# Later slots, an eighth row buffer and a shorter hand-over in a fused conv-attention and mixture-of-experts kernel

## The chip, the core and the metric

One core of a Trainium2 chip runs the kernel. The metric is device time in microseconds (us) of one execution. TensorE is PE in the profile (PEld are its weight loads), VectorE is DVE, ScalarE is ACT, GpSimd is POOL and SyncE is SP. SP only issues DMAs; POOL issues the indirect ones, which scatter or add rows by an index. Each engine and each issuing queue works strictly in order.

## The reference

The input is x of shape (4, 256, 64, 64) in float32, 16384 pixels of 256 channels. Layer 0 adds a 3x3 neighbourhood attention; layer 1 adds a sliding-window attention over tokens and a mixture of experts. What matters here is the mixture:

```python
def _moe(tokens, router_w, w1, b1, w2, b2):
    logits = tokens @ router_w.T
    probs = softmax(logits)
    rw, re = top_k(probs, 2)
    rw = rw / rw.sum(-1, keepdims=True)
    combine = zeros((N, 8)).at[arange(N)[:, None], re].set(rw)
    out = tokens
    for e in range(8):
        h = gelu(tokens @ w1[e] + b1[e], approximate=False)
        out = out + combine[:, e:e + 1] * (h @ w2[e] + b2[e])
    return out

x = x + conv_attention(group_norm(x))
t = to_tokens(x)
t = t + windowed_attention(layer_norm(t))
t = t + moe(layer_norm(t))
```

## The kernel before

The pixels are 32 blocks of 512 tokens (`NB` = 32, eight an image). Two streams run at once.

The **stream of blocks** runs a loop over steps g = 0 to 33. In step g four generators are interleaved: `produce(g + 1)` (queries, scores), `attend(g)` (attention of layer 0, whose first PE work is the transpose `ptp` at L688), `tail(g - 1)` (window attention, norm, choice of experts) and `ranks(g - 2)`. `tail` stores the block's tokens to `out` with SP (`store`, L749). `ranks` counts where each token goes and scatters each token's normed row to `rows_in` in HBM, once for each of its two experts: eight indirect DMAs of 128 rows a block, issued by POOL at L1001.

The **stream of slots** (`experts`) does the mixture for the first 28 blocks. They form 15 groups, numbered from 0: 13 of two blocks, then two of one (`GROUPS`). A group's rows are cut into slots of 256 rows of one expert, 105 in all; group 0 gives 1 slot, groups 1 to 12 give 8 each, the last two 4 each, so the first slots of groups 1 to 5 are 1, 9, 17, 25 and 33. A slot m goes through these steps:

- `fetch` (L1171): SP reads the slot's 256 rows from `rows_in` into a row buffer `sx` of pool `rowp`. It waits until all rows of its group are scattered, and until the buffer is free.
- `matrix`, `pixels`, `hidden`, `output`: the expert's weights are copied by ACT (L1188), the rows transposed on PE (`ptx`, L1195, four instructions), multiplied (`psh`, L1207, and `psy`, L1225, eight each), and bias and gate are applied in place by DVE (L1229, L1230).
- `add` (L1243): the slot's sum. POOL adds the rows into `out` with two indirect DMAs of 128 rows. A sum waits for the landing of the sum before it, and for the group's stores. It frees the row buffer.

A slot is fetched two slots ahead of its transposes. `rowp` has seven buffers, so slot m uses the buffer of slot m - 7. The scattering DMAs are not issued at once: they are put into the list `waiting`, and each sum hands out four or two of them behind itself (`give_rows`); a fetch hands out what is left of its group.

How far the slots have come at each point of the block loop is set by `follow`: at time `at` (in steps) it lets the slots run up to `due`, the lower of two lines of straight pieces, `most` and `wanted`. `most` says that group k begins at `begins[k]`, which is two steps and a lag after the group's last block.

Engines' orders come from the program's order with priorities, so giving out a slot later moves its instructions on every engine.

The last four blocks (28 to 31) are the **tail**: their rows are cut into 53 half slots of 128 rows (`halves`: fetch L1319, transposes L1334, products L1344 and L1360), 21 of which also hold what was left over of the earlier groups. Half slots write their products with POOL to an intermediate `sums_a` (L1373); the 21 add to `out` (L1390). The sums of the last slots of `experts` are held (`HELD` = 4) and put between these, one for every two half slots. At the end `together` reads `sums_a`, adds two rows for each token (L1448) and stores the four blocks.

Of the kernel before, what the change touches and what calls it, by code (L numbers as in the profile page):

```python
# [62 lines left out]
def hybrid_block_kernel(ctx: ExitStack, tc: tile.TileContext, ins: dict, out: bass.AP):  # L63
# [9 lines left out]
    NB = B * NBI  # L73
# [19 lines left out]
    NS = NB - 4  # L93
    GROUPS = (*[2] * 13, *[1] * 2)
    assert sum(GROUPS) == NS
    first_of = [sum(GROUPS[:k]) for k in range(len(GROUPS))]
    where = [(k, j) for k, n in enumerate((*GROUPS, NB - NS)) for j in range(n)]
    APART = len(GROUPS)
# [25 lines left out]
    w2p = ctx.enter_context(tc.tile_pool(name="w2p", bufs=2))  # L124
    w3p = ctx.enter_context(tc.tile_pool(name="w3p", bufs=3))
    w4p = ctx.enter_context(tc.tile_pool(name="w4p", bufs=4))
    rowp = ctx.enter_context(tc.tile_pool(name="rowp", bufs=7))
    w1sp = ctx.enter_context(tc.tile_pool(name="w1sp", bufs=3))
    hbm = ctx.enter_context(tc.tile_pool(name="hbm", bufs=1, space=bass.MemoryType.DRAM))
    ps_a = ctx.enter_context(tc.tile_pool(name="ps_a", bufs=4, space=PSUM))  # L130
# [522 lines left out]
    wxs, sums, table, norm1, x1c = {}, {}, {}, {}, {}  # L653
# [470 lines left out]

    ready = []
    adds = []
    HELD, owed = 4, []
    waiting, given_rows = [], []

    def in_turn(inst, others, own):  # L1130

        for d in others:
            tc.add_manual_dep(
                inst, d.name,
                mybir.DependencyInfo(
                    mybir.DependencyClass.NoSync, mybir.DependencyReason.SCHED_ONLY
                ),
                reason="order of the indirect transfers",
            )
        own.append(inst)  # L1140

    def give_rows(n, k=None):

        while waiting and (n > 0 or k is not None and waiting[0][0] <= k):
            waiting.pop(0)[1]()
            n -= 1

    def experts():
# [86 lines left out]
        def add(m, xs):  # L1235
            k, n = of[m]

            behind = adds[-U:]
            if n == 0:
                at = 1 + sum(GROUPS[:k])  # L1240
                behind = behind + stored[0 if k == 0 else at : at + GROUPS[k]]
            for t in range(U):
                inst = nc.gpsimd.indirect_dma_start(  # L1243
                    out=out, out_offset=bass.IndirectOffsetOnAxis(
                        ap=xs[:, t, C + E : C + E + 1].bitcast(U32), axis=0
                    ),
                    in_=xs[:, t, 0:C], in_offset=None, compute_op=ALU.add,
                ).ins
                tc.declare_no_dep(
                    inst, group="stores", keep=behind, reason="rows of a later group's blocks"  # L1250
                )
                tc.declare_no_dep(
                    inst, group="adds", keep=behind, reason="behind the slot before, no other"
                )
                for d in behind:
                    tc.add_manual_dep(
                        inst, d.name,
                        mybir.DependencyInfo(
                            mybir.DependencyClass.Sync, mybir.DependencyReason.DATA
                        ),  # L1260
                        reason="sums of one row",
                    )
                tc.add_to_no_dep_group("adds", inst)
                in_turn(inst, given_rows[-2:], [])
                adds.append(inst)
            give_rows(4 if len(waiting) > 4 else 2)

        raw = {m: fetch(m) for m in range(FETCH)}
        xcs, hs, done = {}, {}, {}
        for m in range(-2, total + 1):  # L1270
            if FETCH <= m + 2 + FETCH < total:
                raw[m + 2 + FETCH] = fetch(m + 2 + FETCH)
            if m + 2 < total:
                xcs[m + 2] = matrix(m + 2), pixels(m + 2, raw[m + 2])
            yield
            if 0 <= m + 1 < total:
                hs[m + 1] = expert_of(m + 1), hidden(m + 1, *xcs.pop(m + 1))
            yield
            if m > 0:
                sum_ = lambda m=m, xs=done.pop(m - 1): add(m - 1, xs)  # L1280
                if m - 1 < total - HELD:
                    sum_()
                else:
                    owed.append((2.0, sum_))
            if 0 <= m < total:
                yield from output(m, *hs.pop(m), raw.pop(m))
# [171 lines left out]


    STEPS, LAG = {NB: 17, NB + 1: 12}, 0.35  # L1460
    begins = [at + 2 + LAG for at in first_of[1:]] + [NS + 2.0]
    most = [(at, max(0, n - FETCH - 1)) for at, n in zip((*begins, NB + 2.0), (*first_slot, first_slot[-1]))]
    wanted = [(begins[1], 1), *((NB + n, first_slot[-1] - m) for n, m in ((0, 11), (1, 7), (2, 3)))]
    stream, done = experts(), 0
# [17 lines left out]
    for g in range(NB + 2):  # L1482
# [10 lines left out]
        n = 0  # L1493
# [75 lines left out]
```

## Time and profile before

| | |
|---|---|
| median of 3 runs | 1234.81 us (1232.86 to 1239.05) |
| profiled execution | 1238.46 us, of which the span is 1236.8 |
| PE busy | 1106.7 us, 89% of the span |
| DVE, ACT, POOL busy | 917.1, 857.0, 699.5 us |
| sums (L1243), 210 DMAs | 332.9 us of POOL, 1585 ns each |
| rows scattered (L1001), 256 DMAs | 254.6 us of POOL, 995 ns each |
| mean granted clock of TensorE | 0.970 |
| first `sums_a` of the tail (L1373) | at 1081.99 us |

In a line of the timeline the columns are the start in us, the length in us, engine, line, operation, output and inputs, the count, and in brackets the engine's idle time before it with what ended it. In the view by lines, the numbers behind the count are busy us, the mean length in ns, and idle us before with what ended it. In the view of waits they are us in total, times, and the longest. In the windows each engine has its busy us and count; the number behind POOL's count is the granted clock, then come the share of the DMA engines and GB/s. A clock of 1 is full speed.

### The profile page before, as it was taken

The page shows a single profiled execution, that of the slowest core. Times are in us where ns is not written, and L with a number is a line of the kernel's source. Part 1 is how long each engine was busy: PE and PEld are TensorE (multiplying, and loading weights), DVE is VectorE, ACT ScalarE, POOL GpSimd, SP SyncE. Part 2 cuts the span into 40 slices and gives each one's busy share as a digit, 9 for nine tenths or more (in the row PEclk, how much of TensorE's full clock was granted, in tenths as well). Part 3 has the DMA queues.
Part 4 walks back from the last instruction along what each step waited for, and adds up shares of the span by engine and source line. Part 5 has one row for each costly group of instructions (what it writes and reads, how often), then busy time and mean ns, then how long its engine had stood idle before and what let it go on. Part 6 is the DMA issues. An engine that isn't in the chain of part 4 may idle for free. (4 is left out here: it accounts for less than half of the span.)

```text
span 1236.8 us, 29028 instructions
## 1 busy us (share of the span) xinstructions
PE 1106.7 (89%) x8762; PEld 791.4 (64%) x8762; DVE 917.1 (74%) x4632; ACT 857.0 (69%) x1752; POOL 699.5 (57%) x642
## 2 busy tenths in 40 slices
PE   5888889999997969999998999999999999688880
PEld 4544556777775747777666766766666677577670
DVE  4589878888886857888886878888888889234443
ACT  1467679878886757787786887787777766266660
POOL 3113316556553565675665666666566668577772
PEclk9999999999998989999999999999999999799995
DMA  8895548666668577777746786676566456655557
GB/s 277 273 317 172 179 144 244 180 150 157 157 174 159 137 187 199 193 191 198 188 115 163 186 214 166 160 207 156 134 155 154 104 112 148 129 132 118 131 128 233
DMA packets 136146, 214.01 MB, mean 173 GB/s; under 512 B 16368, under 2 KB 102400, under 8 KB 131768
## 3 DMA queue, kind: packets, MB, share of 16 engines
q1 hardware_dynamic: 86264, 137.00, 36.1%
q0 software_dynamic: 48352, 73.05, 29.5%
q10 hardware_dynamic: 1376, 2.10, 0.5%
q8 instruction: 73, 1.20, 0.4%
q14 instruction: 81, 0.66, 0.2%
HBM read 120.78 MB, written 91.31 MB: 171 GB/s over the span
## 5 line engine op out<-in xcount | busy, mean ns | idle before, releaser
L1243 POOL DMA_INDIRECT out<-sx x210 | 332.9, 1585 | 277.8 <-DVE sx L1230 51.3
L1001 POOL DMA_INDIRECT rows_in<-tok,rows x256 | 254.6, 995 | 125.3 <-issue 78.8
L1225 PE MATMUL psy<-w,h 128*128 x840 | 214.1, 386 | 0.4 <-issue 0.2
L1207 PE MATMUL psh<-xc,w1s 128*128 128x256 f32 x840 | 206.2, 387 | 0.0
L1225 PEld LDWEIGHTS psy<-w,h 128*128 128x128 f32 x840 | 153.3, 191 | 50.9 <-issue 24.9
L1207 PEld LDWEIGHTS psh<-xc,w1s 128*128 128x128 f32 x840 | 153.4, 192 | 35.4 <-issue 10.3
L1229 DVE TENSOR_TENSOR sx<-psy,b2b 128x256 f32<-128x256 f32 x210 | 87.7, 417 | 66.3 <-PE psy L1225 60.2
L576 PE MATMUL psq<-x,qks 128*128 128x512 f32 x256 | 124.0, 606 | 1.8 <-ACT qks L497 1.8
L734 PE MATMUL pso<-mixT,vo 128*128 128x512 f32 x256 | 123.5, 605 | 0.0
L1213 ACT ACTIVATE h<-psh,w1s 128x256 f32<-128x256 f32 x210 | 88.1, 471 | 32.0 <-PE psh L1207 30.9
L1195 PE MATMUL ptx<-ident,sx 128*128 128x128 f32 x420 | 66.4, 281 | 31.9 <-DMA sx<-rows_in 31.8
L1199 ACT COPY xc<-ptx 128x512 f32<-128x512 f32 x105 | 61.1, 582 | 47.5 <-PE ptx L1195 47.0
L1195 PEld LDWEIGHTS ptx<-ident,sx 128*128 128x128 f32 x420 | 50.9, 146 | 57.2 <-issue 41.3
L1230 DVE TENSOR_SCALAR sx<-sx 128x256 f32<-128x256 f32 x210 | 78.5, 374 | 2.0
L1213 ACT ACT_TABLE_LOAD x59 | 75.7, 1283 | 0.8
L893 ACT ACTIVATE x<-x,scale 128x256 f32<-128x256 f32 x120 | 63.2, 590 | 18.3 <-DVE scale L867 16.4
L584 ACT ACTIVATE q<-psq,qbb,irc 128x512 f32<-128x512 f32 x64 | 49.9, 779 | 33.1 <-PE psq L576 27.6
L780 PE MATMUL psp<-wpr,x1c 128*128 128x136 f32 x512 | 70.2, 282 | 0.7 <-DVE ispread L473 0.7
L780 PEld LDWEIGHTS psp<-wpr,x1c 128*128 128x128 f32 x512 | 65.5, 190 | 4.8 <-issue 2.1
L576 PEld LDWEIGHTS psq<-x,qks 128*128 128x128 f32 x256 | 45.8, 193 | 34.9 <-issue 33.5
L734 PEld LDWEIGHTS pso<-mixT,vo 128*128 128x128 f32 x256 | 45.5, 190 | 34.3 <-issue 30.1
L1188 ACT COPY w1s<-w1b 128x514 f32 x105 | 65.1, 627 | 2.1 <-issue 0.2
(277 smaller groups left out, 2494.7 us busy)
## 6 DMA issues: line engine op xcount, KB each, us to landing
xp<-in_xp SPq DMA_DIRECT2D x32, 1024.0 KB
sx<-rows_in SPq DMA_DIRECT2D x105, 272.0 KB
x<-in_x SPq DMA_DIRECT2D x32, 660.0 KB
xs<-in_xs SPq DMA_DIRECT2D x32, 512.0 KB
out<-x SPq DMA_DIRECT2D x28, 512.0 KB
sxa<-rows_in SPq DMA_DIRECT2D x32, 136.0 KB
rows_in<-tok,rows POOLq DMA_INDIRECT x256
out<-sx POOLq DMA_INDIRECT x210
```

Source lines behind the costliest of these rows:

```text
L576: inst = nc.tensor.matmul(ps.rearrange("p (r w) -> p r w", w=W), qks[:, ci, co * P : (co + 1) * P], t[:, ci, 1 : TH + 1, 1 : W + 1], start ...
L734: nc.tensor.matmul(ps, vo[:, ci, co * P : (co + 1) * P], mixT[:, ci, :], start=(ci == 0), stop=(ci == NC - 1),)
L780: nc.tensor.matmul(ps[:, u, :], xc[:, ci, t * P : (t + 1) * P], wpr[:, ci, :], start=(ci == 0), stop=(ci == NC - 1),)
L1001: return nc.gpsimd.indirect_dma_start(out=rows_in[:, :], out_offset=bass.IndirectOffsetOnAxis(ap=rows[:, c, t : t + 1], axis=0), in_=tok[: ...
L1188: nc.scalar.copy(w1s, w1b[:, e, :])
L1195: nc.tensor.transpose(pt[:, c, t * P : (t + 1) * P], xs[:, t, c * P : (c + 1) * P], ident)
L1207: nc.tensor.matmul(ps[:, f, :], w1s[:, o : o + P], xc[:, ci, :], start=(ci == 0), stop=(ci == NC - 1),)
L1213: inst = nc.scalar.activation(h[:, f, :], ps[:, f, :], AF.Gelu, bias=w1s[:, F1 + f : F1 + f + 1])
L1225: nc.tensor.matmul(ps, h[:, f, t * P : (t + 1) * P], w2[:, e, f, :], start=(f == 0), stop=(f == NC - 1),)
L1229: nc.vector.tensor_add(ys[:, t, :], ps, b2b[:, e, :])
L1230: nc.vector.tensor_scalar_mul(ys[:, t, :], ys[:, t, :], xs[:, t, bass.ds(e + C, 1)])
L1243: inst = nc.gpsimd.indirect_dma_start(out=out, out_offset=bass.IndirectOffsetOnAxis(ap=xs[:, t, C + E : C + E + 1].bitcast(U32), axis=0), ...
```

## The change

Four numbers or conditions change; no instruction is added to the program or taken out of it.

```diff
-    rowp = ctx.enter_context(tc.tile_pool(name="rowp", bufs=7))
+    rowp = ctx.enter_context(tc.tile_pool(name="rowp", bufs=8))
...
-    HELD, owed = 4, []
+    HELD, owed = 3, []
...
-            give_rows(4 if len(waiting) > 4 else 2)
+            give_rows(4 if len(waiting) > 4 or APART in ready or NB - 1 in sums else 2)
...
-    begins = [at + 2 + LAG for at in first_of[1:]] + [NS + 2.0]
+    begins = [at + 2 + min(LAG * max(n, 1), 1.05) for n, at in enumerate(first_of[1:])] + [NS + 3.0]
```

- `begins`: the lag stays 0.35 of a step for groups 0 and 1, is 0.70 for group 2 and 1.05 from group 3 on; the last knot is at step 31, not 30. In the orders of instructions of both kernels, most of slots 4 to 56 stand later among the blocks on PE than before, and from slot 57 on PE's order is the same.
- `rowp`: eight row buffers, so slot m uses the buffer of slot m - 8.
- `give_rows`: once the last block's ranks are known, a sum hands out four rows. The last block's last four scattering DMAs now stand behind one sum, that of slot 98, where two stood behind 98's and two behind 99's.
- `HELD`: three slots' sums are held for the tail, not four, so the sum of slot 101 stands ahead of the first `sums_a`.

## The prediction

> **What bounds the kernel now.** I read the page's section 1 first, then PE's groups in the view by lines:
>
> ```profile
> PE 1106.7 (89%) x8762; PEld 791.4 (64%) x8762; DVE 917.1 (74%) x4632; ACT 857.0 (69%) x1752; POOL 699.5 (57%) x642
> ```
>
> ```profile
> L1195 PE MATMUL ptx<-ident,sx 128*128 128x128 f32 x420 | 66.4, 281 | 31.9 <-DMA sx<-rows_in 31.8
> ```
>
> PE is busy for 1106.7 of 1236.8 us, and no other engine passes 917.1, so the question is where PE stands idle (last column of the second line). 31.8 us of it stand before the first step of a slot (its transposes, L1195), ended by the fetch of that slot's rows. The timeline of PE gives the large ones:
>
> ```profile
> 380.25 1.09 PE L1195 MATMUL ptx<-ident,sx 128*128 128x128 f32 x4 [6.26 <-DMA sx<-rows_in]
> ...
> 463.04 1.09 PE L1195 MATMUL ptx<-ident,sx 128*128 128x128 f32 x4 [10.38 <-DMA sx<-rows_in]
> ...
> 1059.12 1.09 PE L1195 MATMUL ptx<-ident,sx 128*128 128x128 f32 x4 [8.30 <-DMA sx<-rows_in]
> ```
>
> Counting L1195 in fours, these are slots 25, 33 and 104 (counted from 0). 25 and 33 are the first slots of groups 4 and 5 (counted from 0; group 3 is the fourth). Two smaller waits, 1.36 us at 123 and 4.41 at 168, are slots 0 and 1, which the change does not touch; 0.94 at 436.5 is slot 31. SyncE's waits between 340 and 390, and between 440 and 465, say what the fetches of 25 and 33 waited for:
>
> ```profile
> SPq L1171 <- DMA rows_in<-tok,rows: 19.1, 3, 17.7
> ...
> SPq L1171 <- DMA rows_in<-tok,rows: 17.2, 2, 15.9
> ```
>
> The rows of the group's last block had not been scattered yet. Lastly the windows, whose column behind POOL is the granted clock:
>
> ```profile
> 350.00:400.00 50.00, 43.69 (x343) 30.20 (x341) 35.86 (x190) 36.44 (x72) 25.92 (x22) 0.93 0.71 151
> 400.00:450.00 50.00, 48.84 (x416) 36.07 (x417) 40.37 (x208) 37.66 (x67) 29.00 (x26) 1.00 0.67 179
> 450.00:500.00 50.00, 39.60 (x293) 27.35 (x292) 34.19 (x176) 33.61 (x69) 31.43 (x26) 0.90 0.68 167
> ```
>
> Where PE stood idle, the clock also fell: 7% of 50 us = 3.5 us of full-speed time lost behind the first gap, 10% = 5.0 us behind the second.
>
> **Slots later from group 3 on.** No instruction is added or removed; the order changes. The order of instructions of the two kernels on GpSimd shows after how many slots' sums the last row of a group is handed out. Before: group 4, whose first slot is 25, after 20 sums; group 5 (33) after 28; both 5 slots ahead. The later groups, 41, 49, 57, have a lead of 6, 6 and 7, and none of them stalls PE. Now 25 has its rows after 17 sums, 33 after 26, 41 after 33, 49 after 41, 57 after 49: leads of 7 or 8 everywhere. Is that enough? A slot takes about 8.6 us here (PE's timeline: blocks 11 and 12 begin at 312.3 and 346.6, with four slots between). Two to three slots more of lead are 17 to 26 us, against SyncE waits of 17.7 and 15.9 us and PE gaps of 10.38 at most. So both gaps close, and that of slot 31, whose fetch came late behind the same wait. Worth 6.3 + 3.5 + 10.4 + 5.0 + 0.9 = 26.1 us, since PE is at 50 of 50 us or close to it in the undisturbed windows around.
>
> Moved past on SyncE: loads of x, patches and stores go ahead of one or two fetches more (the store of block 9 stands behind 21 fetches, not 23), which can only bring them earlier.
>
> **Eight row buffers.** SyncE waits 452.8 us in all for sums to land (`out<-sx`) before it may fetch into their buffer, mostly hidden, and everything queued behind on it (stores, loads) waits too. With eight, a fetch waits for the sum one slot older, 8.5 to 10 us earlier. One place where this reaches PE is 663.72: 3.06 us idle and 0.65 at 669, with a clock of 0.97 (1.5 us), behind a store that SyncE issued at 648.93 after two such fetches. That is 5.2 us. Its bounds are 5.2 gained (the store comes earlier) and 5.2 lost (a gap of this size comes up elsewhere); I take 0, as such small gaps hang on several queues. From slot 60 to 95 a fetch is issued over 20 us ahead of its L1195 (926.6 against 947.9 for slot 88), so there the buffer is worth 0. Slot 104 had waited for slot 97's sum; it now waits for 96's, which was issued at 1037.6 and 1039.5, so the 8.30 us gap closes. By itself that is worth 0: 104's own sum is issued at 1106.18 only, behind a full GpSimd queue.
>
> **The last block's rows and three held slots.** GpSimd's timeline around the start of the tail:
>
> ```profile
> 1056.80 1.54 POOL L1243 DMA_INDIRECT out<-sx  x1 [2.87 <-issue]
> ...
> 1068.22 0.98 POOL L1001 DMA_INDIRECT rows_in<-tok,rows  x1 [0.30 <-issue]
> ...
> 1081.99 0.99 POOL L1373 DMA_INDIRECT sums_a<-sxl,to  x1 [8.80 <-DVE sxl L1372]
> ...
> 1112.51 1.60 POOL L1390 DMA_INDIRECT out<-sxl,token  x1 [0.30 <-issue]
> ```
>
> Slot 98's sum starts at 1056.80. Now four rows follow it at 1.29 us each, the last starts at 1064.4 instead of 1068.22, and the half slots can be fetched 3.8 us earlier. Two sums in a row are 6.3 us apart (1050.48 to 1056.80, as each waits for the other's landing), so 99, 100 and 101 start at 1065.7, 1072.0 and 1078.3: slot 101 fills the hole of 8.80 us, where before it came at 1085.31. The first `sums_a` goes out at 1082.2, as before. Then 102 to 104 go in steps of 6.3 from 1084.8, and the first L1390 at 1103.7, 8.8 us earlier, with one pair of `sums_a` (2 x 1.28) fewer behind it: 6.2 us. From there on GpSimd sets the pace: in 1112.5 to 1213.75 it is busy for 74.5 us, and 64 issue gaps of 0.30 make that 93.7 of 101.25. So 6.2 us reach the end. Bounds: 8.8 if the halves are ready in time for all of it, 0 if the removed pair only uncovers PE, which needs about 2 us a half slot against GpSimd's 2.4.
>
> Speaking against it: with slot 104 done earlier, the pauses of 8.30 and 3.80 us in front of the tail (1059.12, 1074.13) become one, and the clock there, already 0.83 in the window 1050 to 1100, could fall for longer. [...] As GpSimd is busy with slot 101 until 1081.9 anyway, my sum leaves it out.
>
> **Sum.** 26.1 + 6.2 = 32.3 us. The profiled execution took 1238.46 us, 3.65 above the median of 1234.81: 1206.2 on its scale, 1202.5 on the runs'.
>
> **Rivals.** (S) Slower: sums that cannot keep up. From step 11 to 22 slots now come at 4 a block, where before it was 3.63 from step 14 on. Slot 17's sum already trails its products by 17 us (332.9 to 349.7), and sums of slots 17 to 24 were 10.0 us apart (349.7 to 419.8), longer than a slot's 8.6. Over 40 slots that adds 56 us of trail. With eight buffers PE is covered for some 46 us (slot 60 begins 56.6 us after slot 52's products; 10 go for sum, landing and fetch). 56 + 17 - 46 = 27 us idle, half as much again for the clock: 40 us, 1242.5. It starts to cost from 9.3 us a sum and eats the whole gain from 9.9. For it: the 10.0. Against it: between slots 33 and 64 sums came every 8.7 us (500.1 to 768.6) with a trail of 6 to 23; and the longest waits (11.58 us idle before 403.45) follow bursts of loads that SyncE let go after the very stalls that go away. [...]
>
> (P) One stall stays: group 5's lead is 7, and slot 27's sum trailed by 32 us (419.0 to 450.9). Its gap and clock come back: 15.4 us, 1218.
>
> (E) PE starves in steps 8 to 11, where 2.8 slots are put off, each of 3.9 us of PE work (4 matmuls that start 0.11 us apart and 16 that start 0.22 apart), and blocks alone cannot fill it (early blocks take 22 us, PE busy for 43 of 50): 11 us, 1213.5. Against: a late step of 31.6 us with 3.63 slots leaves 17.4 to the block, and 17.4 with 2.55 slots is still 27 us of PE work.
>
> (N) Rows ride on the sums of slots, so delaying slots delays their rows as well and the lead is the same: only the tail gains, 1228.6. Against: the orders above.
>
> **Chances.** Forecast 0.62, S 0.13, P 0.12, E 0.06, N 0.07. Range: down to 1194.5 (5.2 and 2.6 more), up to 1226, which takes in P and E and leaves N and S out: 1194 to 1226. About 0.5%, 6 us, can be told from no change: faster 0.80, same 0.08, slower 0.12.
>
> **What would show it.** PE idle before L1195 falls from 31.8 to about 6 us (slots 0 and 1 alone); SyncE's longest wait for `rows_in` at L1171 falls; windows 350 to 500 show a clock of 1.00; block 22's start comes some 26 us earlier; the idle before the first L1373 shrinks from 8.80 to under 1 us, and the first L1390 follows the start of slot 97's sum by 53 us, not 62. I am wrong if PE waits at L1195 for `out<-sx` between steps 14 and 22, or if a gap of 10 us stays at slot 33.

## The result: 1.1% faster, less than half of the forecast

| | before | after |
|---|---|---|
| median, side by side | 1239.05 us (9 runs, 1232.86 to 1244.62) | 1222.21 us (9 runs, 1220.54 to 1229.93) |
| profiled execution, and its span | 1238.46, 1236.8 us | 1222.21, 1220.4 us |
| start to block 7 (its first L688) | 189.5 us | 189.9 us |
| block 7 to block 22 | 503.5 us | 489.3 us |
| block 22 to the sum of slot 97 | 357.5 us | 358.5 us |
| sum of slot 97 to the end | 186.3 us | 182.7 us |

The ratio is 0.9886, with a 95% interval of 0.9863 to 0.991, so the change gains 14.1 us of 1239 (11.2 to 17.0). 32.3 us were forecast. The two profiled spans differ by 16.4 us: +0.4 - 14.2 + 1.0 - 3.6 over the four stretches of the table. The first of the two places that the prediction named gave 14.2 us where it had 26.1, the second 3.6 where it had 6.2.

These stretches come from one execution of each kernel, and the middle one varies. The kernel before and three kernels below that leave its block loop as it is took 498.4 to 503.5 us from block 7 to block 22, 501.0 in the mean; the changed kernel and three with its loop took 488.6 to 492.6, 490.3 in the mean. So about 11 us is a better value for that gain than 14.2.

**The profile after.** The page's busy times, and in the view by lines PE's wait for the rows of a slot:

```profile
PE 1104.9 (91%) x8762; PEld 787.8 (65%) x8762; DVE 916.2 (75%) x4632; ACT 839.8 (69%) x1740; POOL 700.8 (57%) x642
```

```profile
L1195 PE MATMUL ptx<-ident,sx 128*128 128x128 f32 x420 | 64.3, 275 | 7.4 <-DMA sx<-rows_in 7.4
```

The idle time in front of a slot fell from 31.8 to 7.4 us, and that is slots 0 and 1. In PE's timeline slots 25 and 33 start without a pause. In the whole run the fetches of SyncE still wait for scattered rows, but 7.9 us at the longest and 21.6 in all, where it was 17.7 and 93.8:

```profile
393.00 0.60 PE L1195 MATMUL ptx<-ident,sx 128*128 128x128 f32 x4
...
464.92 0.60 PE L1195 MATMUL ptx<-ident,sx 128*128 128x128 f32 x4
```

```profile
SPq L1171 <- DMA rows_in<-tok,rows: 21.6, 10, 7.9
```

The windows of the stretch where the gaps were:

```profile
350.00:400.00 50.00, 48.74 (x400) 35.37 (x399) 42.11 (x217) 37.66 (x74) 29.18 (x26) 1.00 0.71 161
400.00:450.00 50.00, 50.00 (x365) 34.56 (x364) 40.68 (x205) 36.62 (x74) 32.10 (x26) 0.97 0.78 200
450.00:500.00 50.00, 48.86 (x429) 35.49 (x428) 41.26 (x200) 36.88 (x73) 30.33 (x26) 1.00 0.66 168
```

So the gaps that were to vanish have vanished, and the clock is at 1.00 but for 0.97 in the middle window, where PE is busy for all 50 us (the last section looks at that place). Yet block 22 comes only 13.8 us earlier, not 26. The windows from block 7 to block 22 say why; first before, then after:

```profile
189.50:693.00 503.50, 480.98 (x3861) 339.56 (x3859) 407.53 (x2115) 391.38 (x756) 296.53 (x249) 0.98 0.69 174
```

```profile
189.90:679.20 489.30, 480.93 (x3861) 338.98 (x3859) 409.42 (x2115) 374.57 (x744) 294.62 (x249) 1.00 0.70 179
```

PE executes the same 3861 instructions and is busy for the same 481 us, at a mean clock of 0.98 or of 1.00. The whole gain is idle time: 503.5 - 481.0 = 22.5 us before, 489.3 - 480.9 = 8.4 us after. The higher clock shows no gain beside it. And of the 22.5 us, 17.6 before L1195 and 3.1 before L469 are gone (the 3.1 not through the change, as is shown further below), which leaves 1.8: the other 6.6 of the 8.4 us are new. In the view by lines of the two stretches, this is the largest group of it, first before, then after:

```profile
L832 PE MATMUL psg<-wl,bandl 128*64 128x36 f32 x30 | 4.7, 242 | 0.5 <-ACT wl L824 0.5
```

```profile
L832 PE MATMUL psg<-wl,bandl 128*64 128x36 f32 x30 | 4.6, 237 | 4.5 <-ACT wl L824 4.5
```

The tail in GpSimd's timeline after, to set beside the four lines of the prediction, with the sums of slots 100 and 101 (the third and fourth line):

```profile
1044.14 1.56 POOL L1243 DMA_INDIRECT out<-sx  x1 [2.93 <-issue]
...
1051.76 0.96 POOL L1001 DMA_INDIRECT rows_in<-tok,rows  x1 [0.30 <-issue]
...
1060.46 1.53 POOL L1243 DMA_INDIRECT out<-sx  x1 [3.98 <-DMA sxa<-rows_in]
...
1067.48 1.55 POOL L1243 DMA_INDIRECT out<-sx  x1 [3.63 <-DMA sxl<-rows_in]
...
1071.18 0.99 POOL L1373 DMA_INDIRECT sums_a<-sxl,to  x1 [0.30 <-DVE sxa L1372]
...
1094.34 1.60 POOL L1390 DMA_INDIRECT out<-sxl,token  x1 [0.42 <-issue]
```

Slot 97's sum starts at 1037.7. The last rows follow it by 14.0 us (17.7 before), the hole of 8.80 us is 0.30, and the first L1390 comes 56.6 us behind it (62.0 before, 53 forecast).

### The profile page after: what moved, and what is told of

The parts are those of the page before. It is cut to its first block, busy times and chain, and to the rows that moved or that the text cites. A ratio compares the mean times of both kernels' runs of the same rounds, so it can differ in the third digit from the quotient of the medians.

```text
span 1220.4 us, 28993 instructions
## 1 busy us (share of the span) xinstructions
PE 1104.9 (91%) x8762; PEld 787.8 (65%) x8762; DVE 916.2 (75%) x4632; ACT 839.8 (69%) x1740; POOL 700.8 (57%) x642
## 5 line engine op out<-in xcount | busy, mean ns | idle before, releaser
L1225 PE MATMUL psy<-w,h 128*128 x840 | 216.0, 387 | 1.9 <-issue 1.9
L1225 PEld LDWEIGHTS psy<-w,h 128*128 128x128 f32 x840 | 152.1, 190 | 50.2 <-issue 26.3
L1213 ACT ACTIVATE h<-psh,w1s 128x256 f32<-128x256 f32 x210 | 88.2, 470 | 40.7 <-PE psh L1207 39.8
L584 ACT ACTIVATE q<-psq,qbb,irc 128x512 f32<-128x512 f32 x64 | 49.8, 778 | 30.9 <-PE psq L576 25.0
L1195 PE MATMUL ptx<-ident,sx 128*128 128x128 f32 x420 | 64.3, 275 | 7.4 <-DMA sx<-rows_in 7.4
L823 ACT COPY wl<-wx 64x795 f32<-64x795 f32 x32 | 27.3, 852 | 60.9 <-DVE wx L811 60.9
L1195 PEld LDWEIGHTS ptx<-ident,sx 128*128 128x128 f32 x420 | 50.6, 142 | 28.4 <-issue 11.8
```

The source lines that it names most:

```text
L1195: nc.tensor.transpose(pt[:, c, t * P : (t + 1) * P], xs[:, t, c * P : (c + 1) * P], ident)
L1213: inst = nc.scalar.activation(h[:, f, :], ps[:, f, :], AF.Gelu, bias=w1s[:, F1 + f : F1 + f + 1])
L1225: nc.tensor.matmul(ps, h[:, f, t * P : (t + 1) * P], w2[:, e, f, :], start=(f == 0), stop=(f == NC - 1),)
```

## The experiments

All ratios are to the kernel before on the same chip, with 95% intervals. "Middle" is the time from block 7 to block 22 in the profiled execution.

### Which part of the change earns it

Four kernels on one chip. The first three are the kernel before with one part of the change; the fourth is the changed kernel with the old `begins`.

```diff
e1_begins
-    begins = [at + 2 + LAG for at in first_of[1:]] + [NS + 2.0]
+    begins = [at + 2 + min(LAG * max(n, 1), 1.05) for n, at in enumerate(first_of[1:])] + [NS + 3.0]
e1_buf
-    rowp = ctx.enter_context(tc.tile_pool(name="rowp", bufs=7))
+    rowp = ctx.enter_context(tc.tile_pool(name="rowp", bufs=8))
e1_tail
-    HELD, owed = 4, []
+    HELD, owed = 3, []
...
-            give_rows(4 if len(waiting) > 4 else 2)
+            give_rows(4 if len(waiting) > 4 or APART in ready or NB - 1 in sums else 2)
e2_early (against the changed kernel)
-    begins = [at + 2 + min(LAG * max(n, 1), 1.05) for n, at in enumerate(first_of[1:])] + [NS + 3.0]
+    begins = [at + 2 + LAG for at in first_of[1:]] + [NS + 2.0]
```

> The kernel before with the later slots alone (seven buffers, four held sums, old hand-over of rows). Theory M (the lateness of the first slots' rows is the middle's cost, and later slots cure it): PE idle before L1195 falls from 31.8 to about 16 us (slots 0, 1 and 104 stay), block 31 starts 10 to 13 us earlier than in the kernel before, the span falls by 9 to 13 us. Rival R (the eighth buffer is what freed SyncE, and working off the put-off slots at four a block gives the deferral's gain back): block 31 starts at most 5 us earlier.

> The kernel before with eight row buffers alone. Theory M: the first fetches of groups 4 and 5 still wait for rows, so PE idles before L1195 at slots 25 and 33 for 12 to 17 us together; the 8.3 us at slot 104 go, without moving the tail; block 31 starts 0 to 5 us earlier and the span falls by 0 to 5 us. Rival R: 8 us or more.

> The kernel before with three held sums and the new hand-over of rows alone. Nothing before block 31 changes. Theory M: from the start of slot 97's sum to the end of the span it takes 186.3 us in the kernel before and 182.7 in the changed one; here 182 to 184, so the span falls by 2 to 4 us. A rival: slot 104's late fetch (seven buffers) now delays the half slots, and nothing is gained.

> The changed kernel with the slots as early as before (eight buffers and the two changes at the tail stay). Theory M: 3 to 8 us below the kernel before, as the two parts alone add up; the two stalls at slots 25 and 33 are there. Rival R: 11 us or more below, no slower than the changed kernel.

| | median us | ratio | middle us | PE idle before L1195 |
|---|---|---|---|---|
| later slots only | 1224.28 | 0.9896 (0.9863 to 0.9929) | 488.6 | 16.1 |
| eight buffers only | 1236.35 | 1.0004 (0.9978 to 1.0031) | 499.1 | 18.9 |
| tail's two edits only | 1232.88 | 0.9965 (0.9939 to 0.9991) | 498.4 | 30.9 |
| all but the later slots | 1235.24 | 0.9979 (0.9951 to 1.0007) | 503.2 | 23.8 |

The later slots alone are worth 12.9 us (8.8 to 16.9), nearly all of the gain, and without them it is gone. In the kernel with eight buffers only, slot 33 still waits 12.44 us, and the middle is shorter mainly because slot 25's gap happens not to be there. The eighth buffer alone shows no gain (within 3 to 4 us either way); the tail's edits buy 4.3 us (1.1 to 7.5), below the 6.2 forecast but not excluding it.

### How late is late enough

```diff
e2_cap70
-    begins = [at + 2 + min(LAG * max(n, 1), 1.05) for n, at in enumerate(first_of[1:])] + [NS + 3.0]
+    begins = [at + 2 + min(LAG * max(n, 1), 0.70) for n, at in enumerate(first_of[1:])] + [NS + 3.0]
e2_even
-    wanted = [(begins[1], 1), *((NB + n, first_slot[-1] - m) for n, m in ((0, 11), (1, 7), (2, 3)))]
+    wanted = [(begins[1], 1), (begins[3], first_slot[3] - 3), *((NB + n, first_slot[-1] - m) for n, m in ((0, 11), (1, 7), (2, 3)))]
```

> The changed kernel with the lag capped at 0.70 of a step, not 1.05. Rows of groups 4 and 5 are ready 7 and 6 slots ahead (8 and 7 in the changed kernel, 5 and 5 before), and fewer slots are put off: four slots a step only up to step 16, where the changed kernel has them up to step 22. Theory D (working off the put-off slots four a step leaves PE about 1 us idle before L832 in every second step and cost 7 us in the middle): no gap over 3 us at slots 25 and 33, PE idle between blocks 7 and 22 of 3 to 5 us instead of 8.3, and 3 to 5 us below the changed kernel. Rival L (a lead of 7 is needed): a gap of 3 to 10 us is back before slot 33, and it is no faster than the changed kernel.

> The changed kernel with the put-off slots worked off evenly up to step 32: 3.82 a step from step 11 on, instead of 4 up to step 22 and 3.63 behind it. Theory D: steps of exactly four slots become fewer until block 22, so PE's idle there falls to 4 to 6 us; but more pauses come after block 22, and the span is 0 to 4 us below the changed kernel's. Rival: the pauses hang on the order in which the scheduler happens to place them, not on four slots a step, and the idle stays at 8 us or grows.

With half of the added lag, gaps at 25 and 33 stay closed: the lead of slot 33 need not be as long as the change makes it. The small pauses before L832 are gone as well, 0.5 us where the changed kernel has 4.5, as theory D had it. The middle was 487.8 us, with 4.1 us of idle time before L469 (a wait for a store, below). The median, 1226.36 us or 0.9923 (0.9893 to 0.9953), is no better than with the full lag. The profiled execution does not show why: at 1219.48 us it was the fastest of the eight.

Working the put-off slots off evenly up to step 32 (3.82 a step, not 4 up to step 22 and 3.63 behind it) gave 1230.43 us, 0.9963 (0.9942 to 0.9984): 4.6 us of gain are left, about a third. The pauses before L832 fell to 2.0 us, but PE stood idle for 9.63 us at 300.05. In the view of waits between 280 and 320 us, DVE is held by a load of x:

```profile
DVE stats L179 <- DMA xs<-in_xs: 11.2, 1, 11.2
```

SyncE issued that load at 290.86 only, as two fetches ahead of it on its queue had waited (278.87, 11.38 us long). So here a fetch that waited 11.38 us held back the load that stood behind it on SyncE.

### The new small pauses

Before L832 (`psg`, the first products of the window attention) PE waits for the last of three ACT copies that lay out `wl`. ACT's timeline after, at one of these pauses (PE resumes at 476.31 after 0.96 us idle):

```profile
469.57 0.85 ACT L823 COPY wl<-wx 64x795 f32<-64x795 f32 x1 [3.42 <-DVE wx L811]
470.43 1.28 ACT L1213 ACT_TABLE_LOAD   x1
471.73 0.84 ACT L1213 ACTIVATE h<-psh,w1s 128x256 f32<-128x256 f32 x2
472.58 1.28 ACT L634 ACT_TABLE_LOAD   x1
...
475.20 1.06 ACT L824 COPY wl<-wx 64x1060 f32<-64x1060 f32 x1
```

In the new order a slot's gelu (L1213) and the exponentials of the next block's scores (L634), each with a table load of 1.28 us ahead of it, fall between the second copy and the third. The edit puts the three copies first among ACT's ready work:

```diff
e4_wl (against the changed kernel)
+        at = tc.cur_priority
+        tc.cur_priority = 0
         if i == 0:
...
         pace(nc.scalar.copy(wl[0:WIN], wx[0:WIN]))
+        tc.cur_priority = at
e4_cap70_wl: the same, and e2_cap70's line
e7_before_wl: the same in the kernel before
```

> The changed kernel with the two copies of wl (L823, L824) given first place among ScalarE's ready work, so that L824 no longer stands behind two table loads, a gelu pair and four exps. Theory D': L824's place on ScalarE makes the pauses of about 1 us before L832. PE's idle before L832 between blocks 7 and 22 falls from 5.7 us to under 2, and the span by 3 to 6 us. Rival: what is pushed back on ScalarE (gelu or exp) stalls PE elsewhere for as long, and the span stays within 2 us.

> The changed kernel with the wl copies first on ScalarE, beside the one with four held sums on the same chip: 1214 to 1217 us.

> The kernel before with the wl copies (L822 to L824) first on ScalarE, nothing else. Theory: the small pauses before L832 came with the later slots (PE's idle time in blocks 7 to 22 of before is 22.6 us, of which 21.3 are the large gaps), so they earn little here: 1234 to 1240 us, ratio 0.997 to 1.002, the gaps at slots 25 and 33 as before. Rival: the copies save 6 us in any order: ratio 0.995 or less.

With the copies first the changed kernel takes 1216.26 us, 0.9842 (0.982 to 0.9864), and in a second series on another chip 1216.69 us, 0.983 (0.9799 to 0.986): 5 to 7 us better than the changed kernel's 0.9886, and the best version here together with its variant below. PE's idle time before L832 in the middle falls from 4.5 to 0.4 us (the 5.7 of the expectation is the sum up to block 31), its whole idle time there to 484.9 - 481.6 = 3.3 us, and the window between 305.8 and 679.2 has PE at 372.2 of 373.4 us, where the changed kernel has 367.7.

In the kernel before, the same edit gave 1236.84 us, 0.9962 (0.9936 to 0.9988): 4.7 us, 1.5 to 7.9, more than expected of it. Its profile shows about 2 us of that behind block 22, where either kernel gains the same (284.8 to 283.0 us from block 22 to 31 before, 285.4 to 282.8 after). In the middle it is 4.3 us shorter, but slot 25's gap was 2.67 us in that execution and not 6.26, which accounts for 3.6, a chance of that execution as far as the runs tell. So of the 5 to 7 us that the copies bring in the changed kernel, 4.4 (489.3 to 484.9) belong to pauses that came with the later slots, and some 2 were there to be had before.

### Stores behind fetches

> Both: the lag capped at 0.70 and wl's copies first on ScalarE. Theories D and D' together: 5 to 9 us below the changed kernel, 1213 to 1217. If the pauses come from one cause, no more than the better of the two parts.

That kernel took 1223.73 us, 0.9916 (0.9885 to 0.9946), against 1216 with the full lag. Its middle has PE idle for 10.94 us at one place, before L469 at 655.66, and ACT's waits between 630 and 690 us name the cause:

```profile
ACT x L768 <- DMA out<-x: 13.5, 1, 13.5
```

ACT may overwrite `x` only when the store of the old one has landed. SyncE's timeline has that store behind two fetches that had waited for sums (this kernel has three more lines behind L824, so L1174 is the fetch):

```profile
626.64 11.95 SPq L1174 DMA_DIRECT2D sx<-rows_in  x2
638.69 0.41 SPq L152 DMA_DIRECT2D xp<-in_xp  x1
639.20 0.42 SPq L749 DMA_DIRECT2D out<-x  x1
```

At this place the kernel before idled for 3.06 us (the prediction's 663.72) and the changed kernel not at all. Other profiles of these same orders gave 0 to 3.7 us (below), so a share of the 10.9 may be chance. To take the store out of the queue, three kernels issue the loop's stores from ACT's queue:

```diff
e6_st (against the changed kernel), e6_wl_st (against e4_wl), e6_cap70_wl_st (against e4_cap70_wl)
-        inst = nc.sync.dma_start(
+        inst = (nc.scalar if g < NS else nc.sync).dma_start(
```

> The changed kernel with the token stores of the loop (L749) issued from ScalarE's queue, not SyncE's. Theory S: the stall before gm (L469) near block 21 comes from stores that stand on SyncE behind fetches that wait for sums; in the changed kernel that stall is 0 to 1.4 us already, so little is to be gained here: 1217 to 1224 us, no idle over 1.5 us before PE's first work after gm of an image. Rival A: ScalarE's queue pays for the issue, as the store waits there for its tokens with all later copies behind it: 32 stores with 0.3 us or more each in front of PE, 1230 us or more.

> The same on the kernel that also has the wl copies (L822 to L824) ahead of the exponentials on ScalarE. Theory S: equal to that kernel's 1216 us within 4 us, as its stall was already absent. Rival A: 1224 us or more.

> The lag capped at 0.70, wl copies first, and the stores on ScalarE's queue. Without the stores moved, this order lost 10.9 us of PE idle and about 2 us of clock at one store that SyncE issued late behind fetches waiting for sums. Theory S: the stall goes and the time falls from 1223.7 to 1210 to 1214 us, the middle (block 7 to 31) from 777 to about 765. Rival A: the stall goes but ScalarE pays, 1220 us or more. Rival B: the stall's cause is the landing of the store and not its issue; it stays at 10 us and the time at 1223.

| | median us | ratio | middle us | PE idle in it |
|---|---|---|---|---|
| changed kernel, stores on ACT | 1232.79 | 0.996 (0.994 to 0.998) | 494.0 | 12.2 |
| copies first, stores on ACT | 1231.86 | 0.9955 (0.9936 to 0.9975) | 489.6 | 9.4 |
| lag 0.70, copies first, stores on ACT | 1227.4 | 0.9915 (0.9885 to 0.9945) | 485.4 | 5.8 |

In the third, ACT waits no longer for the store, and the middle falls from 494.3 to 485.4 us: with SyncE's timeline above, that makes the store's place in SyncE's queue the cause. But the time does not fall, and in the other two kernels, whose profiles have no such stall without the edit, it rises, by the ratios, by 9 and 14 us. Within the middle 4.7 us of it are found in each (489.3 to 494.0, 484.9 to 489.6): PE now waits 5.5 and 7.9 us before L721 for work that passes through DVE and ACT, where it waited for under 0.7 in either kernel with the stores on SyncE. So ACT's part of the block pays. It pays behind block 22 too: from there to slot 97's sum the three kernels take 362.7, 360.8 and 360.9 us, and 358.5, 354.9 and 354.7 with the stores on SyncE. That is 4 to 6 us in each, also in the third. Block 7 begins at 194.7 to 197.5 us in all three; whether the edit does that or the spread of starts (last section) is not told apart.

### The tail's two edits apart

```diff
e3_held4 (against the changed kernel), e7_wl_held4 (against e4_wl)
-    HELD, owed = 3, []
+    HELD, owed = 4, []
e3_rows (against the changed kernel)
-            give_rows(4 if len(waiting) > 4 or APART in ready or NB - 1 in sums else 2)
+            give_rows(4 if len(waiting) > 4 else 2)
```

> The changed kernel with four slots' sums held for the tail, as before, not three. If the three held sums are worth the 2.6 us of one pair of sums_a fewer ahead of the first L1390, and the filled hole, the end comes 3 to 5 us later relative to slot 97's sum (186 to 188 us, not 182.7) and the time is 1225 to 1227 us; idle before the first sums_a (L1373) comes back to 6 to 9 us. If the tail is bound by something else (PE, or the transfers), the end relative to slot 97's sum stays within 1.5 us of 182.7.

> The changed kernel with give_rows as before (the last block's last rows behind two sums). Theory: the four-row hand-over is what the tail earned, 3 us: last row 17 to 18 us after slot 97's sum, not 14.0, the end 185 to 187 us after it, not 182.7, and 1225 us. Rival: the tail is paced by its products and transfers; the end stays within 1.5 us of 182.7 and the time at 1222.

> The changed kernel with the wl copies first on ScalarE and four held sums, not three. If the three held sums earn what the prediction put down for them, 2.6 us and more: 1219 to 1221 us against 1216.3 with three. If they earn nothing, 1214 to 1217 us and the end 178 to 181 us after slot 97's sum.

| | median us | ratio | slot 97's sum to the end |
|---|---|---|---|
| changed kernel | 1222.21 | 0.9886 (0.9863 to 0.991) | 182.7 us |
| four sums held | 1224.65 | 0.9901 (0.9865 to 0.9937) | 180.2 us |
| old `give_rows` | 1224.89 | 0.9883 (0.985 to 0.9916) | 179.6 us |
| copies first, four held (beside 1216.69 with three) | 1216.48 | 0.9813 (0.979 to 0.9837) | 180.8 us |

Neither edit shows a gain on top of the other, and both theories miss: with four held sums the idle time before the first `sums_a` is 1.05 us and not 6 to 9, and with the old `give_rows` the last row comes 17.9 us behind slot 97's sum, as expected, but the end 179.6 us and not 185 to 187. The profiles show why. Each edit by itself takes away the hole of 8.80 us: 1.05 us of it remain with the four-row hand-over alone, 0.96 with three held sums alone, 0.30 with both. The first L1390 starts 60.9 to 62.2 us behind slot 97's sum in the four kernels with the old tail, and 57.9, 55.2 and 56.6 us behind it in these three. What remains from there to the end takes 119.7 to 126.1 us over all profiles, a spread larger than these differences.

Over all profiles, kernels with seven buffers and the old tail end 183.6 to 186.3 us after slot 97's sum (three kernels), those with eight buffers or with the edits of the tail 178.3 to 183.3 (fifteen); eight buffers alone give 181.8. The profiles of one and the same kernel, copies first, gave 178.3 and 181.8, so a split of these 3 to 4 us among the three edits stays open.

## Why the prediction was half right

**Later slots: the mechanism held, the term was mis-sized.** The gaps of slots 25, 31 and 33 closed, and 17.6 us of idle time with them, as the forecast's 6.3, 10.4 and 0.9 had it. Rivals S and P, with new waits or one left, did not come: in the middle no idle time before L1195 is left, and the sums of slots 17 to 24 came 9.1 us apart (10.0 before), those of 33 to 64 8.6, below the 9.3 from which S was to cost. Of rival E's 11 us, 3.2 of idle time stand in blocks 8 to 11. Rival N is excluded by the gaps having closed. That the measured time lies in the range of 1194 to 1226 us is luck all the same: its upper end stood there for P and E, which did not come, and what took the time back was in no rival. (The lower end by the prediction's own numbers is 1194.7, not 1194.5.) Two steps of the sum failed.

*"7% of 50 us = 3.5 us of full-speed time lost behind the first gap, 10% = 5.0 us behind the second."* These 8.5 us were not there. Finer windows of the kernel before, around the two gaps:

```profile
377.00:380.20 3.20, 0.00 (x0) 0.00 (x0) 0.00 (x0) 1.26 (x7) 1.74 (x2) 0.51 0.83 197
380.25:384.00 3.75, 3.75 (x16) 1.67 (x16) 1.25 (x6) 1.21 (x2) 0.00 (x0) 0.52 0.92 255
384.00:388.00 4.00, 4.00 (x21) 3.08 (x18) 3.68 (x20) 2.79 (x5) 1.81 (x2) 1.00 0.92 219
452.60:463.00 10.40, 0.07 (x2) 0.00 (x0) 4.06 (x25) 2.48 (x8) 8.28 (x8) 0.64 0.63 123
463.04:466.00 2.96, 2.96 (x11) 2.41 (x12) 0.00 (x0) 1.10 (x2) 0.61 (x2) 0.54 0.99 263
```

Read as a mix of a clock of 1.00 and one of 0.50, an estimate from these rows, the stretches around the two gaps hold about 17 us at half clock, and some 10.7 of them lie inside the pauses (3.20 us at 0.51, 10.40 at 0.64), where PE has next to nothing to do: that time was already counted as the gap. Behind the pauses PE ran at 0.52 for 3.75 us and at 0.54 for 2.96, so at most 1.8 + 1.4 = 3.2 us of full-speed time were lost. Even these do not show in the sum, as PE's busy time in the middle is 481 us in both kernels, and between 479.5 and 481.6 in twelve more profiles with the same instructions there (3860 or 3861) and a mean clock of 0.98 to 1.00.

*"since PE is at 50 of 50 us or close to it in the undisturbed windows around"*: true of before, not of the new order. 8.4 us of idle time stand in its middle, 6.6 of them new: 4.0 more before L832 (0.5 to 4.5), and 1.3 each before L1225 (0.4 to 1.7) and L968 (0.0 to 1.3). The prediction costed the move at nothing on the other engines; on ACT it put a gelu and four exponentials with two table loads ahead of a copy that PE needs. The copies-first kernel shows that for the pauses before L832 by removing them; 1.3 us before L968 stay in it. The pauses before L1225 vary between 0.5 and 1.7 us in the four kernels with this order.

**The clause on small stalls.** The 3.06 us at 663.72 were put at 0, bounds 5.2 either way. They went in this profile, worth 3.1 us, but that was chance and not the change. Up to block 22 the kernels with four held sums and with the old `give_rows` have the changed kernel's order on every engine, and they idle there for 3.68 and 2.17 us; the kernel with the tail's two edits alone has the order of the kernel before, and does not idle there. Over all kernels above it was 0 to 10.9 us, so bounding was right and 5.2 too narrow.

So the middle of this pair of profiles is -17.6 - 3.1 + 6.6 = -14.1 us against 14.2 measured, where the forecast had -26.1.

**Eight buffers at 0** agrees with the run (1.0004, within 3 to 4 us either way).

**The tail: 3.6 us, not 6.2.** Rows 3.7 us earlier and the filled hole came as forecast, though either edit fills the hole alone. What failed is the chain "99, 100 and 101 start at 1065.7, 1072.0 and 1078.3", in steps of 6.3 us. Measured from slot 98's, the steps to 99, 100, 101 and 102 are 8.9, 7.4, 7.0 and 7.4 us: the first contains the four rows and is as forecast, and in front of 100 and 101 GpSimd stands idle for 3.98 and 3.63 us, where in a row of sums before it was 2.87. The profile ends both idle times with a landing of a half slot's rows; that the sums' landings were stretched beside those fetches is my reading and was not tried. So the first `sums_a` came 33.4 us after slot 97's sum, not 31.7, and the first L1390 gained 5.4 us, not 8.8. From there to the end the changed kernel takes 126.1 us and the kernel before 124.3, which is 1.8 more where the sum had 2.6 for the pair of `sums_a` that moves behind it. "From there on GpSimd sets the pace" does not hold by itself: the kernel with eight buffers alone gives GpSimd the same instructions in the same order there as the kernel before, and took 119.7 us. What else sets the pace stays open.

**The longer pause.** The prediction weighed that the clock could fall for longer behind one long pause in front of the tail. The pause came (10.28 us before the first L1334), and the half slots behind it ran at a granted clock of 0.50. But so they did in the kernel before, behind its pause of 3.80 us. The windows from the first L1334 on, first before, then after:

```profile
1074.10:1080.20 6.10, 5.73 (x24) 5.23 (x25) 0.28 (x2) 2.72 (x8) 0.00 (x0) 0.50 0.78 199
```

```profile
1057.60:1063.50 5.90, 5.90 (x24) 5.23 (x25) 0.26 (x2) 2.75 (x8) 2.73 (x2) 0.50 0.84 204
```

Both kernels pay for about 6 us at half clock here, with the same 24 instructions, so the longer pause shows no further cost, and leaving it out of the sum was right.

## What to carry to other kernels

A mean clock over a window that holds a pause need not be a second loss beside the pause (here 8.5 us were read from it, and PE's busy time was 481 us with the pauses and without): take the clock from the work behind the pause only, or compare PE's busy time over a stretch with the same instructions, and price the rest as idle time. When a step is moved to close a wait on one queue, read the order of every other engine at the new place, above all a copy that the critical engine needs and that can slip behind table loads (two of 1.28 us here). Between two profiles, compare stretches that begin at the same block, as starts differ, and look at a second profile with the same order before a small difference is given a cause: the same orders took 498.4 and 503.5 us, and 489.3 to 492.6, in the middle.

## What the runs showed of the hardware

The first 190 us differ from execution to execution by up to 10 us, as much as the longest gap that the change closed (10.38). Block 7 began between 187.8 and 197.9 us over the eighteen profiles. In the kernel with the old `give_rows`, whose instructions on PE up to block 7 are those of the changed kernel, it came 8.0 us later than there. Here are the windows of 30 to 190 us, first of the changed kernel, then of that one:

```profile
30.00:190.00 160.00, 135.36 (x1371) 79.38 (x1371) 123.83 (x706) 104.61 (x242) 41.24 (x53) 0.97 0.66 218
```

```profile
30.00:190.00 160.00, 137.03 (x1347) 79.17 (x1347) 119.08 (x684) 97.25 (x227) 38.19 (x50) 0.91 0.62 204
```

PE is busy for longer and has done less (1347 instructions, not 1371), at a granted clock of 0.91 and not 0.97. In the six profiles with 0.97 or 0.98 in this window block 7 began at 187.8 to 191.6 us, in the four with 0.91 to 0.93 at 194.5 to 197.9. What sets the clock of a start is not shown: no run here changes it by itself.

The granted clock also fell where PE had hardly paused. These are windows of the changed kernel, around the one in the middle whose clock was 0.97:

```profile
397.80:401.20 3.40, 2.40 (x29) 2.26 (x30) 2.69 (x16) 1.98 (x3) 1.86 (x3) 1.00 1.04 372
401.30:404.70 3.40, 3.40 (x7) 1.85 (x6) 2.42 (x13) 1.70 (x3) 0.00 (x0) 0.50 0.53 88
```

The only pause shortly ahead of the half clock is one of 1.18 us, which ended at 398.80. So in this execution a pause of 1.18 us, far shorter than the gaps, was followed by 3.4 us at a clock of 0.50.
